# Cross-attention kernel: twelve value loads issued by GpSimd, and other slots for the loads of the first batch

## Chip, cores, metric

The kernel runs on one core of a Trainium2 chip. The metric is the device time of one execution in microseconds (us). Engines: TensorE (PE in the profile: matrix products), VectorE (DVE), ScalarE (ACT), GpSimd (POOL) and SyncE (SP), which only issues transfers. Each engine works through its own instructions in order; engines wait for each other by semaphores. Transfers (DMA) are issued by SyncE or by GpSimd, each into its own queue, and are carried by 16 DMA engines.

## What is computed

```python
# x: (8, 256, 1024), ctx: (8, 256, 1024), 32 heads of 32, all float32
h = (x - mean(x)) * rsqrt(var(x) + 1e-5) * gamma + beta
Q = split_heads(h @ Wq.T)              # K = V = split_heads(ctx)
scores = einsum('bhsd,bhtd->bhst', Q, K) * 32 ** -0.5
scores = where(mask, scores, -inf)
probs = softmax(scores)
attn = einsum('bhst,bhtd->bhsd', probs, V)
out = x + merge_heads(attn) @ Wout.T
```

## The kernel before

Work goes in **quads**: four heads of one batch, 8 quads a batch, 64 in all, numbered n = 0 to 63. The main loop has one iteration per quad; iteration n computes the scores of quad n+1 on TensorE, then its softmax, and the values product (probabilities times V, `values`, L823) of older quads. Between these stand the query products of the next batch, the output products of the last one, and the preparation of later batches: load of x, statistics (`ln_stats`), normalisation (`ln_norm`), block transposes (`blocks_x`), sixteen moves between partitions (`move_x`). The order on each engine is the order in which the Python program issues the instructions; it is written out by hand, and a table `PLAN` at the top of the file says in which iteration ("slot") each load, sum and move stands and which engine does it.

**Softmax of a quad** (`softmax_parts`, L663): for each of its four heads VectorE adds the mask and takes the row maximum (L687), ScalarE takes the exponential and its sum (L691), VectorE the reciprocal (L701), GpSimd the scaling (L707; fifty heads of the plan are scaled by ScalarE, L705), VectorE a transpose by blocks (L713). ScalarE copies one half aside (L719, `pc`), and four transfers swap quarters between partitions (L793): two `pT<-pT`, and, once these have landed, two `pT<-pc`. Only then is a quad's `pT` ready for the values product. Loads of the iteration come in two lists: `ahead`, issued right after the last normalisation of the softmax and ahead of the swaps, and `between`, issued between the two pairs of swaps. For quads 1 to 7, and again in the last batch, the last transpose, the swaps and `between` are held back into the next quad's softmax (`tails`).

**Values.** From quad 8 on, V of two quads (n, n+1; 512 KB) comes by one load (`load_v`, L286) into one buffer, `v_all`, which there is once (`vp`: 1). For quads 8 to 53 the plan's `pairs` lets odd iterations run the values products of two quads together (`values_pair(n - 3)`), and `vlate` puts the load of quads n, n+1 (n from 8 to 54) into `ahead` of iteration n+1, that is right behind the products that read the buffer before. It must have landed two iterations later; for quad 54, which is worked alone, one. Quads 0 to 7 have a load of 256 KB each, into one half of the buffer; quads 56 to 63 use another buffer.

**Who issues a load.** Every load, move and store has a key, and `issue` (L247) looks it up in the plan's `qp`: 0 (not listed) is SyncE (L252), 1 is GpSimd at that place of the program (L254), 2 is GpSimd at the end of the iteration (L1323). Loads of values of quads 24 to 55 share keys by their number modulo 8, since `per(n)` gives "%0" to "%7" there; `v%0` is listed with 1, so quads 24, 32, 40 and 48 are loaded by GpSimd.

**The first batch.** `woload` lists loads of output weights as [which, pair, slot]: `which` is 0 for the block B11, 1 for B21, 2 for B22, 3 for B12; a slot below 0 is before the loop, behind the loads of query weights. In slots 3 and 4 the two loads of B21 are added. Sums of these blocks run on GpSimd from slot 4 on. `b2` holds the slots of batch 2's preparation: loads, statistics, norms and transposes of the two halves of x, and the sixteen moves. `rs0` holds the slots of the four loads of residual rows of batch 0, counted from 8; the rows are used by VectorE and GpSimd in iterations 10 to 14. All these loads stand in `between`.

```python
ahead = [partial(load_v, n)] if ... and n not in V_EARLY and str(n) not in V_LATE else []
if V_LATE.get(str(n - 1)) == 'a':
    ahead.append(partial(load_v, n - 1))
...
for load in ahead:
    load()
```

Of the kernel before, what the change touches and what calls it, by code (L numbers as in the profile page):

```python
# [53 lines left out]
 'folds': 'PPPPPPPP',  # L54
 'b2': {'loads': [0, 1],
        'stats': [2, 4],
        'norms': [2, 4],
        'trans': [3, 5],
        'moves': [5, 5, 5, 5, 5, 5, 5, 6, 6, 6, 6, 6, 7, 7, 7, 7]},
 'b3': {'loads': [-14, -11],  # L60
        'stats': [-10, -9],
        'norms': [-9, -8],
# [11 lines left out]
         'norms': [-9, -8],  # L74
         'trans': [-8, -7],
         'moves': [-7, -6, -6, -6, -6, -6, -6, -5, -5, -5, -4, -4, -4, -4, -4, -4]},
 'woload': [[2, 1, 0], [3, 0, 3], [0, 1, 1], [0, 0, 3], [3, 1, 2], [2, 0, 2]],
 'n11': 'V',
 'p1late': [0],
 'qp': {'out00': 2,  # L80
# [39 lines left out]
        'x2_0None': 1,  # L120
        'ring3_B110': 2,
        'mv2_11': 1,
        'r1_11': 2},
 'vearly': {'62': 'b', '60': 'z'},
 'rs': [0, 1, 1, -3],
 'rs0': [-1, 1, 1, 1],
 'bufs': {'ptp': 4, 'vp': 1, 'asp': 2},
 'vsplit': 8,
 'pairs': [11, 13, 15, 17, 19, 21, 23, 25, 27, 29, 31, 33, 35, 37, 39, 41, 43, 45, 47, 49, 51, 53, 55],
# [1302 lines left out]
```

## Time and profile before

| | us |
|---|---|
| plain runs, median of 3 | 580.47 (579.62 to 581.26) |
| profiled execution, its time | 583.7 |
| profiled execution, span from first to last instruction | 581.9 |

Times in the profile count from the first instruction. A row of the timeline has the start, the length, the engine, the line, the operation, written and read tiles, shapes, the number of instructions merged, and in brackets how long the engine had stood idle and what ended that. `SPq` marks SyncE's issues: the length is the issue's own, not the transfer's. `pv` is the result of the values product, `wo` output weights, `ring` and `kept` parts of weights moved out and in, `sc` scores, `r` residual rows, `xnT<-xe` the moves of x.

### The profile page before, as it was taken

How to read it: one execution, taken by the hardware profiler on the slowest of the kernel's cores; microseconds unless marked ns; L12 is line 12 of the kernel's file. 1: busy time of each engine (PE TensorE's matmuls, PEld its weight loads, DVE VectorE, ACT ScalarE, POOL GpSimd, SP SyncE). 2: the span in 40 equal slices, each digit the busy share in tenths (PEclk: the TensorE clock that was granted, in tenths of full speed). 3: DMA queues.
4: the chain of work that ended last, by engine and by line, in shares of the span. 5: the costliest groups of instructions: out<-in, count | busy, mean ns of one | idle time of the engine just before them, and what ended most of it. 6: DMA issues, size and time to landing. Idle time of an engine off the chain costs nothing.

```text
span 581.9 us, 19975 instructions
## 1 busy us (share of the span) xinstructions
PE 566.3 (97%) x7162; PEld 397.5 (68%) x7162; DVE 463.4 (80%) x1700; ACT 450.5 (77%) x1524; POOL 397.2 (68%) x637
## 2 busy tenths in 40 slices
PE   8999899999999999999999999999899999999997
PEld 8787776766676777577666776677566776754543
DVE  5899888888888799898788888888856879679823
ACT  4699988887798977888678897789668788879920
POOL 1579987869867886967577673877916865257680
PEclk9999999999999999999999999999989999999999
DMA  8578967766876778777885788867785666645651
GB/s 315 215 203 231 264 181 212 203 179 168 239 220 200 200 204 261 213 202 201 226 245 162 205 240 235 241 171 192 174 239 154 206 179 200 160 113 164 188 159 74
DMA packets 45908, 116.94 MB, mean 201 GB/s; under 512 B 9136, under 2 KB 9904, under 8 KB 45808
## 3 DMA queue, kind: packets, MB, share of 16 engines
q1 hardware_dynamic: 39808, 96.50, 58.9%
q0 software_dynamic: 5712, 19.14, 11.0%
q8 instruction: 57, 0.93, 0.7%
q14 instruction: 43, 0.35, 0.2%
q10 hardware_dynamic: 288, 0.01, 0.0%
HBM read 64.23 MB, written 11.53 MB: 130 GB/s over the span
## 4 chain that ended last, share of the span: by engine, by line
PE 59%; DMA 12%; DVE 9%; ACT 7%; POOL 5%; issue 4%; SPq 3%; DVEq 0%; POOLq 0%
PE po_S L923 13%; PE pq_A L608 9%; PE po_A L923 8%; PE pv L833 8%; PE sc L647 7%; PE pq_S L608 6%; PE pq L506 6%; DMA pT<-pT 5%; DVE e L687 4%; DMA v_all<-in_kv_dram 4%; POOL e L707 4%; ACT e L691 4%; PE po_end L990 2%; DVE pT L713 2%; SPq L252 2%
## 5 line engine op out<-in xcount | busy, mean ns | idle before, releaser
L707 POOL TENSOR_SCALAR e<-e,rden 128x256 f32<-128x256 f32 x412 | 191.6, 480 | 135.3 <-DVE rden L701 129.5
L691 ACT ACTIVATE e<-e,mn 128x256 f32<-128x256 f32 x512 | 253.8, 503 | 29.9 <-DVE mn L687 29.2
L713 DVE STREAM_TRANSPOSE pT<-e 128x512 f32<-128x512 f32 x256 | 180.8, 708 | 52.9 <-POOL e L707 26.9
L687 DVE CUSTOM_DVE_ANT_0 e<-sc,mb 128x256 f32<-128x256 f32 x512 | 185.3, 415 | 13.2 <-PE sc L647 12.3
L719 ACT COPY pc<-pT 128x512 f32<-128x512 f32 x128 | 78.8, 617 | 47.2 <-DVE pT L713 32.1
L691 ACT ACTIVATION_READ_ACCUMULATOR e<-e,mn 128x1 f32 x512 | 99.4, 194 | 0.0
L506 PE MATMUL pq<-xnT,wq 128*128 128x256 f32 (+1 forms) x368 | 84.0, 382 | 0.0
L506 PEld LDWEIGHTS pq<-xnT,wq 128*128 128x128 f32 x368 | 68.8, 190 | 14.7 <-issue 4.4
L647 PE MATMUL sc<-k,qa 32*128 32x256 f32 x1024 | 73.8, 401 | 0.1
L923 PE MATMUL po_S<-wo,at 128*128 128x512 f32 x152 | 73.7, 606 | 0.2 <-ACT ends L941 0.2
L647 PEld LDWEIGHTS sc<-k,qa 32*128 32x128 f32 x1024 | 45.9, 184 | 39.4 <-issue 21.1
L833 PE MATMUL pv<-pT,v_all 64*32 64x128 f32 x3584 | 62.9, 278 | 7.6 <-DMA v_all<-in_kv_dram 4.9
L833 PEld LDWEIGHTS pv<-pT,v_all 64*32 64x32 f32 x3584 | 53.7, 107 | 19.7 <-issue 8.7
L923 PE MATMUL po_A<-wo,at 128*128 128x512 f32 x128 | 58.5, 602 | 0.1
L701 DVE RECIPROCAL rden<-den 128x2 f32<-128x2 f32 x256 | 38.0, 148 | 22.1 <-ACT e L691 21.8
L923 PE MATMUL po_S<-wo,s 128*128 128x512 f32 x104 | 49.3, 605 | 0.2 <-DVE r L965 0.2
L705 ACT ACTIVATE e<-e,rden 128x256 f32<-128x256 f32 x100 | 45.0, 501 | 1.6 <-DVE rden L701 1.6
L608 PEld LDWEIGHTS pq_A<-xnT,wq 128*128 128x128 f32 x352 | 41.0, 192 | 5.3 <-issue 4.5
L923 PEld LDWEIGHTS po_S<-wo,at 128*128 128x128 f32 x152 | 26.0, 190 | 24.2 <-issue 23.6
L687 DVE DVE_READ_ACCUMULATOR2_ANT mn<- 128x1 f32 x512 | 42.4, 83 | 0.0
L923 PEld LDWEIGHTS po_A<-wo,at 128*128 128x128 f32 x128 | 23.3, 190 | 26.9 <-issue 23.8
L608 PE MATMUL pq_A<-xnT,wq 128*128 128x128 f32 x352 | 41.1, 275 | 0.0
(116 smaller groups left out, 682.6 us busy)
## 6 DMA issues: line engine op xcount, KB each, us to landing
pT<-pT SPq DMA_DIRECT2D x128, 128.0 KB, 3.7
pT<-pc SPq DMA_DIRECT2D x128, 128.0 KB, 3.6
v_all<-in_kv_dram SPq DMA_DIRECT2D x19, 512.0 KB, 5.3
k<-in_kv_dram SPq DMA_DIRECT2D x31, 256.0 KB, 4.2
r<-in_x_dram SPq DMA_DIRECT2D x26, 256.0 KB, 4.4
ring<-kept_T SPq DMA_DIRECT2D x11, 512.0 KB, 5.3
xnT<-xe SPq DMA_DIRECT2D x76, 64.0 KB, 3.3
out_dram<-r POOLq DMA_DIRECT2D x18, 256.0 KB, 3.6
```

The lines of the kernel that those rows point to most:

```text
L506: nc.tensor.matmul(pqs[n], wq[:, o, c, :], xnTs[b](c), start=(c == 0), stop=(c == NC - 1),)
L608: nc.tensor.matmul(pqs[b][:, o, :], w[:, c], x_[:, c], start=begins and o + c == 0, stop=c == NK - 1, skip_group_check=True,)
L647: nc.tensor.matmul(scs[n][j][:, s, :], qa[r, n % NQ, ts(s, P)], ks[n - n % 2][r, n % 2, :], start=True, stop=True,)
L687: nc.vector.tensor_tensor_reduce(out=e[:, s, :], in0=pss[j][:, s, :], in1=mbs[n // NQ], scale=1.0, scalar=NO_SCORE, op0=ALU.add, op1=ALU.m ...
L691: nc.scalar.activation(e[:, s, :], e[:, s, :], AF.Exp, bias=mn[:, s : s + 1], scale=-1.0, accum_out=den[:, s : s + 1],)
L701: nc.vector.reciprocal(rden, dens[j])
L705: engine.activation(es[j][:, s, :], es[j][:, s, :], AF.Copy, scale=rden[:, s : s + 1])
L707: engine.tensor_scalar(es[j][:, s, :], es[j][:, s, :], rden[:, s : s + 1], 1.0, ALU.mult, ALU.mult,)
L713: nc.vector.transpose(pT[:, :, :, j, :, :].rearrange("p a i s k -> p (a i) s k"), es[j].rearrange("p s (b t) -> p b s t", t=K),)
L719: nc.scalar.copy(pc[:, :, ts(j, 2)], pT[:, 1, :, ts(j, 2)])
L833: nc.tensor.matmul(pvs[n][r][j * HD : (j + 1) * HD], vs[n - n % 2][ts(r, 2 * K), n % 2, i, ts(j, HD)], pT[ts(r, 2 * K), :, i, j, :, :], st ...
L923: nc.tensor.matmul(po, operand(b, name)[:, c], wo[:, which, c], start=begins and c == 0, stop=c == NK - 1, skip_group_check=not begins,)
```

## The change

Only the table `PLAN` changes; the program that reads it is the same. The values of quads 26, 28, 30, 34, 36, 38, 42, 44, 46, 50, 52 and 54 (with the quad after each) are issued by GpSimd. Of the output weights' loads, B12's first pair goes from slot 3 to before the loop, B12's second from slot 2 to 1, B22's second from slot 0 to 2. The second half of batch 2's x is loaded in slot 0 (was 1), its statistics and norm stand in slot 3 (was 4), the first half's transpose in slot 4 (was 3); of the moves, six, six and four stand in slots 5, 6 and 7 (were seven, five and four). The residual rows of batch 0 are loaded in slots 8, 8, 10 and 11 (were 7, 9, 9 and 9).

```diff
- 'b2': {'loads': [0, 1],
-        'stats': [2, 4],
-        'norms': [2, 4],
-        'trans': [3, 5],
-        'moves': [5, 5, 5, 5, 5, 5, 5, 6, 6, 6, 6, 6, 7, 7, 7, 7]},
+ 'b2': {'loads': [0, 0],
+        'stats': [2, 3],
+        'norms': [2, 3],
+        'trans': [4, 5],
+        'moves': [5, 5, 5, 5, 5, 5, 6, 6, 6, 6, 6, 6, 7, 7, 7, 7]},
...
- 'woload': [[2, 1, 0], [3, 0, 3], [0, 1, 1], [0, 0, 3], [3, 1, 2], [2, 0, 2]],
+ 'woload': [[0, 0, 3], [3, 1, 1], [3, 0, -1], [0, 1, 1], [2, 0, 2], [2, 1, 2]],
...
-        'r1_11': 2},
+        'r1_11': 2,
+        'v%2': 1,
+        'v%4': 1,
+        'v%6': 1},
...
- 'rs0': [-1, 1, 1, 1],
+ 'rs0': [0, 0, 2, 3],
```

## The prediction

> **What bounds the kernel now.** I read the page's engine sums first, then the groups of TensorE, then TensorE's timeline for every place where it stood still.
>
> ```profile
> span 581.9 us, 19975 instructions
> PE 566.3 (97%) x7162; PEld 397.5 (68%) x7162; DVE 463.4 (80%) x1700; ACT 450.5 (77%) x1524; POOL 397.2 (68%) x637
> L833 PE MATMUL pv<-pT,v_all 64*32 64x128 f32 x3584 | 62.9, 278 | 7.6 <-DMA v_all<-in_kv_dram 4.9 <-DMA pT<-pT 1.5 <-ACT e L705 1.0
> ```
>
> TensorE is busy for 566.3 of 581.9 us, so no edit of loads can win more than its idle 15.6 us (and what its clock loses). Half of that, 7.6 us, stands ahead of one group: the values products, mostly for the value load. One by one, with the stall in brackets:
>
> ```profile
> 59.65 1.25 PE L833 MATMUL pv<-pT,v_all 64*32 64x128 f32 x64 [0.48 <-DMA pT<-pT]
> 68.37 1.25 PE L833 MATMUL pv<-pT,v_all 64*32 64x128 f32 x64 [1.01 <-ACT e L705]
> 84.60 1.26 PE L833 MATMUL pv<-pT,v_all 64*32 64x128 f32 x64 [0.98 <-DMA v_all<-in_kv_dram]
> 282.16 2.31 PE L833 MATMUL pv<-pT,v_all 64*32 64x128 f32 x128 [0.98 <-DMA pT<-pT]
> 368.40 2.20 PE L833 MATMUL pv<-pT,v_all 64*32 64x128 f32 x128 [0.91 <-DMA v_all<-in_kv_dram]
> 402.19 2.13 PE L833 MATMUL pv<-pT,v_all 64*32 64x128 f32 x128
> 422.46 3.87 PE L833 MATMUL pv<-pT,v_all 64*32 64x128 f32 x128 [2.33 <-DMA v_all<-in_kv_dram]
> 501.79 1.36 PE L833 MATMUL pv<-pT,v_all 64*32 64x128 f32 x64 [0.66 <-DMA v_all<-in_kv_dram]
> 422.80:426.20 3.40, 3.40 (x127) 0.50 0.84 234
> ```
>
> The first three are quads 3, 4 and 6; then come the pairs that begin with quads 28, 38 and 44, and quad 54. The last row (a window of TensorE: length, busy, granted clock, DMA share, GB/s) shows that after the 2.33 us stop the clock stood at 0.50 for 3.40 us, which costs half of it, 1.70 us: that pair took 3.87 us where an undisturbed one takes 2.13.
>
> **Why these loads are late.** A value load waits only for the pair before it to be read. SyncE issued those loads here:
>
> ```profile
> 277.29 0.53 SPq L252 DMA_DIRECT2D v_all<-in_kv_dram  x1
> 362.96 0.40 SPq L252 DMA_DIRECT2D v_all<-in_kv_dram  x1
> 410.79 3.67 SPq L793 DMA_DIRECT2D pT<-pc  x2
> 414.50 2.46 SPq L252 DMA_DIRECT2D xnT<-xe  x3
> 417.00 0.58 SPq L252 DMA_DIRECT2D v_all<-in_kv_dram  x1
> 497.22 0.54 SPq L252 DMA_DIRECT2D v_all<-in_kv_dram  x1
> ```
>
> For quad 44 the buffer was free at 402.19 + 2.13 = 404.32, but the load stood behind the swaps of another quad (410.79) and three moves, and went out at 417.00, 12.7 us later. Nothing about its own data held it.
>
> **The change: values of quads 24 to 55.** Twelve loads (26, 28, 30, 34, 36, 38, 42, 44, 46, 50, 52, 54) leave SyncE; the four at multiples of 8 were GpSimd's already. In GpSimd's order each stands right behind the normalisation of the quad two ahead, as the trace shows for a load that it has now (219.25 + 1.85 = 221.10, load at 221.04):
>
> ```profile
> 219.25 1.85 POOL L707 TENSOR_SCALAR e<-e,rden 128x256 f32<-128x256 f32 x4 [0.53 <-DVE rden L701]
> 221.04 0.58 POOL L254 DMA_DIRECT2D v_all<-in_kv_dram  x1
> 268.29 2.88 POOL L707 TENSOR_SCALAR e<-e,rden 128x256 f32<-128x256 f32 x6 [0.55 <-DVE rden L701]
> 358.21 0.94 POOL L707 TENSOR_SCALAR e<-e,rden 128x256 f32<-128x256 f32 x2 [4.27 <-ACT e L705]
> 407.22 2.89 POOL L707 TENSOR_SCALAR e<-e,rden 128x256 f32<-128x256 f32 x6 [0.54 <-DVE rden L701]
> 495.79 0.94 POOL L707 TENSOR_SCALAR e<-e,rden 128x256 f32<-128x256 f32 x2 [0.83 <-DVE rden L701]
> ```
>
> So the new issue times are 271.2, 359.2, 410.1 and 496.7: earlier by 6.1, 3.8, 6.9 and 0.5 us. Time from issue to landing, loads of SyncE from 232 us on, then those of GpSimd from 205 us on (minimum, median, maximum):
>
> ```profile
> DMA to landing us min/median/max: 4.1/5.3/8.6
> DMA to landing us min/median/max: 3.8/4.7/5.9
> ```
>
> With 4.7 us they land at 275.9, 363.9, 414.8 and 501.4. TensorE was ready at 281.18, 367.49, 420.13 and 501.13 (start less stall), so the first three stalls go: 0.98 + 0.91 + 2.33 = **4.2 us**, and the half clock with them, **1.7 us**. Quad 54 keeps 0.3 of 0.66: **0.4 us**. What is late next there: for quad 45 the swap back, of which the second went out near 414 and landed after some 3.6 us, ahead of 420.13; so I let TensorE run on.
>
> ```profile
> pT<-pc SPq DMA_DIRECT2D x128, 128.0 KB, 3.6
> DVE pT L713 <- POOL e L707: 26.9, 94, 1.4
> ```
>
> Twelve issues like that at 221.04, 0.58 us each, add 7.0 us to GpSimd. Behind each wait the sums for the products and the next quad's normalisation, and for that VectorE's transposes, which wait for GpSimd 26.9 us in all now. I cost it at nothing: the cover is GpSimd's 32% idle and the lead of several us that transposed probabilities have on TensorE. Without it the price is up to 0.58 us a load, 7.0 in all. SyncE gains 12 x 0.53 = 6.4 us, which I also count as nothing. Where SyncE was prompt the new issue is later, and this bounds the edit from the other side:
>
> ```profile
> 318.29 2.11 PE L833 MATMUL pv<-pT,v_all 64*32 64x128 f32 x128
> 323.42 0.53 SPq L252 DMA_DIRECT2D v_all<-in_kv_dram  x1
> 324.50 0.94 POOL L707 TENSOR_SCALAR e<-e,rden 128x256 f32<-128x256 f32 x2 [1.01 <-DVE rden L701]
> 333.45 1.79 PE L833 MATMUL pv<-pT,v_all 64*32 64x128 f32 x106
> ```
>
> Quad 34 (and alike 26, 42, 50, once per batch): buffer free at 320.40, SyncE at 323.42, GpSimd at 325.4; needed at 333.45. There is room for 8.0 us of landing, against 4.7 at the median and 5.9 at most for GpSimd. I take no loss.
>
> **The change: the head.**
>
> ```profile
> 20.00:25.00 5.00, 5.00 (x35) 3.87 (x34) 4.15 (x13) 1.73 (x5) 3.19 (x7) 1.00 0.34 136
> 55.00:60.00 5.00, 4.52 (x50) 3.49 (x56) 4.88 (x19) 3.81 (x14) 4.37 (x10) 1.00 1.04 227
> 55.38 2.29 SPq L252 DMA_DIRECT2D wo<-in_woT_dram  x3
> 60.29 1.15 SPq L793 DMA_DIRECT2D pT<-pc  x2
> 70.97 5.19 SPq L252 DMA_DIRECT2D xnT<-xe  x7
> 76.26 1.16 SPq L793 DMA_DIRECT2D pT<-pT  x2
> 81.26 0.54 SPq L252 DMA_DIRECT2D v_all<-in_kv_dram  x1
> 60.15 1.24 ACT L413 ACTIVATE x<-x,shift,rstd 128x1024 f32<-128x1024 f32 x1 [1.04 <-POOL shift L410]
> ```
>
> One 512 KB load of output weights moves from the group of three at 55.38 to the end of the loads before the loop, where the DMA engines then work at 0.34 (20 to 25 us) and not at 1.04 (55 to 60). In between, x and weights only trade places: one such load per quad either way. At 227 GB/s the 0.52 MB less is 2.3 us less queue ahead of quad 4's swap back (60.29) and its value load, so its stall of 1.01 goes if that were all. But the second half of batch 2's x is now normalised a quad earlier, 1.24 us on ScalarE ahead of quad 5's exponentials and the swap of quad 4, which gives part back: I take 0.6. Moves in the first group fall from seven to six: at 5.19 / 7 = 0.74 us each that swap (76.26) and quad 6's value load (81.26) come earlier by at least that, and by the shorter queue before them: 0.9 of the 0.98. Quad 3's 0.48 stays. Head: **1.5 us**; bounds 2.0 (both stalls) and a loss of 1.2 (the ScalarE step on the path). The residual rows (before: one at quad 7's slot, three at quad 9's; after: two at 8, one each at 10 and 11) still have about two quads, some 15 us, against 8.6 us for the slowest of the larger loads above, and cost nothing; without that lead it would be one wait of that order.
>
> **Sum.** 4.2 + 1.7 + 0.4 + 1.5 = 7.8 us off the profiled execution's own 583.7 us: 575.9. That execution is 3.2 us over the median of the plain runs, 580.47. The item that is likeliest to be a matter of one execution is quad 44's stop with its half clock, 4.0 us; without it 3.8 us remain, 576.7 from the median; with it 572.7. I take **575.8**, nearer the former, since 583.7 - 4.0 = 579.7 is about what the plain runs show. Own range 572.5 to 578.5.
>
> **Rivals.**
> 1. Head worth nothing or a small loss, values as forecast. For it: ScalarE's added 1.24 us; against: the DMA share of 1.04. 580.47 - (0.98 + 0.91 + 0.4) = 578.2, or 574 with quad 44's; say 577.5.
> 2. The waits only change their name: the load is early and the swaps, or a normalisation delayed by 0.6 us, end at the same moment. For it: the stall at 282.16 is put down to a swap. Against: the swaps' lead worked out above. 580.
> 3. Slower: the loads of the four short intervals come late. Each has 8.0 us; past that TensorE waits once per batch. SyncE's loads took up to 8.6, GpSimd's up to 5.9, so the row is against it. At 9.8 us it would be 4 x 1.8 = 7.2 us, less 2.1 for the small stalls cured: 585.5; with nothing else gained it turns to a loss from 8.5 us on.
> 4. Slower: the head's ScalarE step and a shifted queue cost 2 us or more, and the plain runs never had quad 44's stop: 582.5.
>
> The Trainium skill speaks for the third (SBUF — State Buffer, "SBUF: two separate sides"): descriptors of a load issued from GpSimd are written by GpSimd, which certain VectorE operations lock out; its example grows from 620 to 3100 ns. By that, an estimate, a load would land 2.5 us later, at about 7.2 us, still short of 8.0. The trace does not agree so far: the loads from GpSimd landed no later than SyncE's.
>
> **How the numbers follow.** Forecast 0.52, rivals 0.16, 0.12, 0.12, 0.08. From no change one can tell 0.3%, 1.7 us: faster is below 578.7, slower above 582.2. The forecast and most of the first rival are faster: 0.64; the second and their edges the same: 0.16; the third and fourth slower: 0.20. The range 572.5 to 583.0 leaves out the third rival and a gain beyond all stalls, under 2 in 10.
>
> **What would show it.** Right: no stall at the pairs of quads 28, 38 and 44, value loads issued within 7 us of the pair's end, no window at half clock, seven 512 KB value loads left on SyncE, the stalls of quads 4 and 6 under 0.5 us. Wrong: stalls at the pairs of 26, 34, 42 or 50, GpSimd's loads landing after more than 8 us, or VectorE's wait for GpSimd growing by more than 7 us with TensorE idle for scores.

## The result, and the profile after

| | before | after |
|---|---|---|
| plain runs on one chip, median of 22 each (us) | 579.9 (577.25 to 588.23) | 577.35 (575.28 to 580.62) |
| ratio of the runs, 95% interval | | 0.9951 [0.9932, 0.9970] |
| profiled execution: time, span (us) | 583.7, 581.9 | 577.82, 576.0 |

The change makes the kernel faster by 0.5%, 2.8 us in plain runs (the forecast was 4.7). The ratio goes by the means of the runs without the few executions in a slower state, so it differs a little from that of the medians, which lie 2.55 us apart. In the code after the change, lines stand three lower than before: the values products of L833 are L836, SyncE's issue of L252 is L255. Some of the kernels below shift by none or by up to six lines; the texts of the rows say which step is meant.

From the page of the kernel after: the span, the engine sums, the group of the values products and the issues of value loads by GpSimd.

```profile
span 576.0 us, 19987 instructions
PE 566.6 (98%) x7162; PEld 397.0 (69%) x7162; DVE 463.1 (80%) x1700; ACT 449.3 (78%) x1524; POOL 402.9 (70%) x649
...
L836 PE MATMUL pv<-pT,v_all 64*32 64x128 f32 x3584 | 60.9, 273 | 0.8 <-ACT e L708 0.8
...
v_all<-in_kv_dram POOLq DMA_DIRECT2D x17, 512.0 KB, 5.1
```

TensorE's work is the same (566.6 against 566.3 us busy), so the span fell by idle time. Ahead of the values products 0.8 us of it is left, of 7.6. The timeline, load and product in turn, for the pairs that begin with quads 28, 38 and 44, and for quad 54:

```profile
271.31 0.58 POOL L257 DMA_DIRECT2D v_all<-in_kv_dram  x1
280.36 2.11 PE L836 MATMUL pv<-pT,v_all 64*32 64x128 f32 x128
...
356.55 0.59 POOL L257 DMA_DIRECT2D v_all<-in_kv_dram  x1
365.91 2.11 PE L836 MATMUL pv<-pT,v_all 64*32 64x128 f32 x128
...
407.44 0.61 POOL L257 DMA_DIRECT2D v_all<-in_kv_dram  x1
416.49 2.12 PE L836 MATMUL pv<-pT,v_all 64*32 64x128 f32 x128
...
489.34 0.60 POOL L257 DMA_DIRECT2D v_all<-in_kv_dram  x1
493.82 1.39 PE L836 MATMUL pv<-pT,v_all 64*32 64x128 f32 x64
```

None of these products has a bracket any more: each load now goes out some 9 us ahead of its use (4.5 for quad 54), and the pair of quad 44 takes 2.12 us where it took 3.87, with no stop and no half clock before it.

One stop is new in this execution, at quad 61 near the end. The timeline, and TensorE's window behind it (length, busy and counts of PE, PEld, DVE, ACT, POOL, then granted clock, DMA share, GB/s):

```profile
534.50 1.11 SPq L807 DMA_DIRECT2D x_again<-in_x_dram  x2
...
538.41 1.15 SPq L796 DMA_DIRECT2D pT<-pc  x2
...
545.66 2.06 PE L836 MATMUL pv<-pT,wq 64*32 64x128 f32 x64 [1.88 <-DMA wq<-in_kv_dram]
```

```profile
546.30:549.70 3.40, 3.40 (x64) 1.98 (x42) 0.00 (x0) 2.21 (x6) 3.37 (x5) 0.51 0.65 149
```

The bracket names a load of values that had gone out at 532.64, but the product begins 0.14 us behind the landing of the first swap back. The swaps back issued from 538.41 on landed at 545.5 and 545.9: after 7 us, behind the 1 MB of `x_again` that SyncE had issued 4 us ahead of it. The stop of 1.88 us was again followed by 3.40 us at half clock.

Twelve more issues on GpSimd were to cost nothing. Of the waits in the kernel after, VectorE's transposes for GpSimd (sum, count, longest):

```profile
DVE pT L716 <- POOL e L710: 29.2, 75, 4.4
```

It was 26.9 before and is 26.6 in the kernel that has only the values edit, so the 2.3 us more do not come from these issues. The experiments say where they come from.

### The profile page after: what moved, and what is told of

Read it like the earlier page. It is cut to its first block, busy times and chain, and to the rows that moved or that the text cites. A ratio compares the mean times of both kernels' runs of the same rounds, so it can differ in the third digit from the quotient of the medians.

```text
span 576.0 us, 19987 instructions
## 1 busy us (share of the span) xinstructions
PE 566.6 (98%) x7162; PEld 397.0 (69%) x7162; DVE 463.1 (80%) x1700; ACT 449.3 (78%) x1524; POOL 402.9 (70%) x649
## 4 chain that ended last, share of the span: by engine, by line
PE 66%; DVE 9%; POOL 8%; ACT 5%; issue 5%; DMA 5%; SPq 2%; DVEq 0%; POOLq 0%; ACTq 0%
PE po_S L926 15%; PE pq_A L611 13%; PE pv L836 8%; PE sc L650 8%; PE po_A L926 7%; PE pq L509 6%; POOL e L710 5%; PE pq_S L611 5%; DVE e L690 4%; PE po_end L993 3%; ACT e L694 3%; DVE pT L716 2%; DMA pT<-pT 2%; DMA xnT<-xe 1%; SPq L255 1%
## 5 line engine op out<-in xcount | busy, mean ns | idle before, releaser
L710 POOL TENSOR_SCALAR e<-e,rden 128x256 f32<-128x256 f32 x412 | 190.4, 476 | 118.8 <-DVE rden L704 112.8
L716 DVE STREAM_TRANSPOSE pT<-e 128x512 f32<-128x512 f32 x256 | 180.7, 708 | 58.0 <-POOL e L710 29.2
L836 PE MATMUL pv<-pT,v_all 64*32 64x128 f32 x3584 | 60.9, 273 | 0.8 <-ACT e L708 0.8
L836 PEld LDWEIGHTS pv<-pT,v_all 64*32 64x32 f32 x3584 | 51.7, 105 | 12.7 <-issue 8.2
L926 PEld LDWEIGHTS po_A<-wo,at 128*128 128x128 f32 x128 | 23.3, 190 | 26.9 <-issue 25.0
```

The lines of the kernel that those rows point to most:

```text
L710: engine.tensor_scalar(es[j][:, s, :], es[j][:, s, :], rden[:, s : s + 1], 1.0, ALU.mult, ALU.mult,)
L716: nc.vector.transpose(pT[:, :, :, j, :, :].rearrange("p a i s k -> p (a i) s k"), es[j].rearrange("p s (b t) -> p b s t", t=K),)
L836: nc.tensor.matmul(pvs[n][r][j * HD : (j + 1) * HD], vs[n - n % 2][ts(r, 2 * K), n % 2, i, ts(j, HD)], pT[ts(r, 2 * K), :, i, j, :, :], st ...
L926: nc.tensor.matmul(po, operand(b, name)[:, c], wo[:, which, c], start=begins and c == 0, stop=c == NK - 1, skip_group_check=not begins,)
```

## Experiments

Each ratio is against the kernel before, run on the same chip among the runs of its group; the medians of before were 580.45, 581.02 and 581.62 us for the first four kernels, the next four and the last four.

### The two halves of the change alone

`values_only`: the kernel before with the three keys `v%2`, `v%4`, `v%6`. `head_only`: the rest of the change without them.

```diff
-        'r1_11': 2},
+        'r1_11': 2, 'v%2': 1, 'v%4': 1, 'v%6': 1},
```

> The kernel before with only the twelve value loads issued by GpSimd; the head as before. Theory (each part brings its own): the stalls of the pairs of quads 28, 38 and 44 and the half clock go, those of quads 3, 4 and 6 (0.48, 1.01, 0.98 us) stay; ratio to the kernel before 0.996 to 0.998 in plain runs. Rival (the gain came from the head, the loads only changed the name of the wait): the pairs' stalls go but swaps or scores stop TensorE by as much; ratio 0.999 to 1.001. Rival (loads from GpSimd late in the short intervals): stalls at the pairs of quads 26, 34, 42 or 50, ratio over 1.

> The kernel before with only the head's slots changed (weights, rows, batch 2's x); values of quads 24 to 55 as before. Theory: stalls of quads 3, 4 and 6 fall from 2.5 us in all to about 0.8, the pairs of quads 28, 38 and 44 still stop TensorE by 1 to 4 us in all; ratio 0.997 to 0.999. Rival (the head brings nothing): ratio 1.000 and the same three stalls.

Measured: values_only 575.66 us, ratio **0.9911 [0.9882, 0.9941]**, which is 5.2 us less; head_only 582.81 us, ratio **1.0044 [1.0021, 1.0067]**, 2.6 us more. Neither expectation was met (0.996 to 0.998 and 0.997 to 0.999). The two add up to the change (0.9951). So the values edit alone is better than the whole, and the head, which was to gain 1.5 us, costs 2.6.

Where does the head lose? Not at its own place. In all four kernels run so far that have the head's new slots (after, head_only and the two of the next parts) TensorE stops at 170 to 175 us, ahead of the first query product of batch 3 (`pq_S`). The timeline of values_only, then of head_only: SyncE's swaps of quad 15, GpSimd's load of the second half of batch 4's x, GpSimd's first sum of batch 3's moved x, VectorE's and ScalarE's steps behind it, and the product.

```profile
142.83 1.14 SPq L796 DMA_DIRECT2D pT<-pT  x2
143.60 0.60 POOL L1326 DMA_DIRECT2D x<-in_x_dram  x1
145.07 1.28 SPq L796 DMA_DIRECT2D pT<-pc  x2
...
161.39 1.29 POOL L599 TENSOR_TENSOR sx<-xnT 128x512 f32<-128x512 f32 x1 [3.31 <-DMA pT<-pc]
...
164.98 0.71 DVE L716 STREAM_TRANSPOSE pT<-e 128x512 f32<-128x512 f32 x1 [1.39 <-POOL e L710]
...
168.25 0.48 ACT L522 ACTIVATE qa<-pq,qa 128x256 f32<-128x256 f32 x1
...
170.93 3.73 PE L611 MATMUL pq_S<-sx,ring 128*128 128x128 f32 x32
```

```profile
143.06 0.60 POOL L1323 DMA_DIRECT2D x<-in_x_dram  x1
143.79 1.15 SPq L793 DMA_DIRECT2D pT<-pT  x2
149.08 1.25 SPq L793 DMA_DIRECT2D pT<-pc  x2
...
161.99 1.52 SPq L252 DMA_DIRECT2D xnT<-xe  x1
...
165.37 1.26 POOL L596 TENSOR_TENSOR sx<-xnT 128x512 f32<-128x512 f32 x1 [7.84 <-DMA pT<-pc]
...
168.92 0.71 DVE L713 STREAM_TRANSPOSE pT<-e 128x512 f32<-128x512 f32 x1 [5.88 <-POOL e L707]
...
169.71 0.91 ACT L705 ACTIVATE e<-e,rden 128x256 f32<-128x256 f32 x2 [4.03 <-DVE rden L701]
...
171.91 0.46 ACT L519 ACTIVATE qa<-pq,qa 128x256 f32<-128x256 f32 x1
...
172.51 3.81 PE L608 MATMUL pq_S<-sx,ring 128*128 128x128 f32 x32 [1.43 <-POOL shift L410]
```

The swaps back (`pT<-pc`) go out only when the first swaps have landed. In values_only that is 2.2 us behind them, in head_only 5.3, and there the 512 KB load of x stands in front of the swaps. Behind the swaps back in SyncE's order stand the last moves of batch 3's x; the last goes out at 161.99 (158.56 in values_only). GpSimd waits for it, 7.84 us instead of 3.31. The bracket of the sum names a swap back; but the sum reads what the moves write, and in the eleven traces that have the landing of that last move it begins 0.38 to 0.39 us behind it.

How the late sum stops TensorE takes a closer look, since the sums themselves end at 167.97, 4.5 us before the product begins. Behind its sums GpSimd does its scalings of the softmax. VectorE's transposes wait for those (5.88 us instead of 1.39), so its reciprocals `rden` come late, and ScalarE waits for them 4.03 us. Behind that stands ScalarE's copy `qa<-pq,qa`. It reads out the query product before this one, and the program has one buffer for these results (`ps_q`), so the new product must wait for it. The copy ends at 172.37 (at 168.73 in values_only, well ahead of the product), and in all six traces with the stop TensorE's wait for ScalarE ends 0.03 to 0.04 us behind this copy. The bracket at the product names GpSimd's `shift` instead, which ends 0.07 to 0.08 us behind the copy in the same six traces; the product reads nothing of `shift`. VectorE's longer waits for GpSimd in the kernel after, 29.2 us, come from here too: the longest of them, 4.4 us, ends at 167.30.

### The same value loads, later on GpSimd

`values_end` is the kernel after with the twelve loads at the end of GpSimd's iteration.

```diff
-        'v%2': 1, 'v%4': 1, 'v%6': 1},
+        'v%2': 2, 'v%4': 2, 'v%6': 2},
```

> The changed kernel with the twelve loads issued by GpSimd at the end of the iteration, behind its sums, and not right behind the normalisation. Theory (what counts is when the load goes out): issue 8 to 9 us after the buffer is free and not 5, so in the short intervals (quads 26, 34, 42, 50) landing at 13 to 14.5 us against 13.1 needed: stalls of 0 to 1.5 us there, ratio 0.996 to 1.000. Rival (what counts is that SyncE is rid of the loads): no new stalls, ratio as for the changed kernel, 0.994 to 0.996.

Measured: 582.36 us, ratio 1.0031 [1.0000, 1.0061]. The timeline of values_end, and TensorE's window behind the product:

```profile
365.24 0.55 POOL L1326 DMA_DIRECT2D v_all<-in_kv_dram  x1
...
372.69 3.53 PE L836 MATMUL pv<-pT,v_all 64*32 64x128 f32 x128 [2.51 <-issue]
```

```profile
373.20:376.60 3.40, 3.40 (x118) 3.02 (x98) 0.81 (x7) 0.36 (x3) 2.50 (x4) 0.50 0.74 194
```

The load of quad 38 went out at 365.24 (356.55 in the kernel after), and the stop with its half clock is back. Same engine, same twelve loads, another place: what the values edit gains is the earlier time of issue, not that GpSimd does it. The stops did not come where they were expected: the pairs of 26, 34, 42 and 50 have none, those of 30, 38 and quad 54 have 1.44, 2.51 and 1.32 us. And the loads are not the whole of the difference, since this profile also stops 1.67 us ahead of `pq_S` (0.47 after).

### The stop at quad 61

`again_early` is the kernel after with `x_again` loaded four iterations earlier.

```diff
-        if n == N - 4:
+        if n == N - 8:
```

> The changed kernel with the second load of the last batch's x (x_again, two of 512 KB) in iteration 56 and not 60. Theory (the changed kernel gives part of its gain back in the tail, where these loads stand between the two pairs of swaps of quad 61): the swaps back of quad 61 land some 3 us earlier, the stop of 1.88 us at quad 61 and the half clock behind it (1.7 us) go; span about 573, ratio 0.990 to 0.993. Rival (that stop was one execution's): the profile has no such stop but the plain runs stay at 0.994 to 0.996.

Measured: 581.16 us, ratio 0.9995 [0.9965, 1.0026]. The stop at quad 61 was gone, as expected, but the time did not fall (0.990 to 0.993 was expected): TensorE now waited 1.23 us for a load of K at 523.78. The larger lesson is in the kernels that leave the end as it was: none of the other twelve profiles shows a stop over 0.52 us at quad 61. The stop belonged to one execution, and there was next to nothing to win. The profile of again_early shows the stop at batch 3's product larger than after, though both have the same instructions up to there:

```profile
143.84 0.60 POOL L1326 DMA_DIRECT2D x<-in_x_dram  x1
144.27 1.15 SPq L796 DMA_DIRECT2D pT<-pT  x2
...
174.70 3.48 PE L611 MATMUL pq_S<-sx,ring 128*128 128x128 f32 x29 [1.86 <-POOL shift L413]
```

### Which of the head's edits

Four kernels: the change with the residual rows in their old slots (`rows_back`), and the values edit with one of the head's three edits each.

```diff
rows_back   (after)         - 'rs0': [0, 0, 2, 3],     + 'rs0': [-1, 1, 1, 1],
values_rows (values_only)   - 'rs0': [-1, 1, 1, 1],    + 'rs0': [0, 0, 2, 3],
values_wo   (values_only)   woload as after
values_b2   (values_only)   b2 as after
```

The theory here was that the rows, loaded two and three slots later, push SyncE back.

> The kernel after with the four residual rows of batch 0 back in slots 7, 9, 9, 9. Theory (rows): the rows at slots 10 and 11 delay SyncE, batch 3's last move goes out some 3 us later, GpSimd waits for it (6.37 us idle at 163.74 in the kernel after, 3.31 with the values edit alone), and TensorE stops before the first query product of batch 3. With the rows back that stop near 170 us is gone, GpSimd's wait is 3 to 4 us, and the ratio to the kernel before is 0.988 to 0.991: the gains of the weights' and x slots at quads 4 and 6 come on top of the values edit's 0.991. Rival (x and moves of batch 2, or the weights' loads): the stop stays, ratio 0.993 to 0.997.

> The values edit and the residual rows' new slots, the rest of the head as before. Theory (rows): the stop at the first query product of batch 3 is there, 0.4 to 1.8 us, GpSimd's wait before it is over 5 us, ratio 0.994 to 0.999. Rival: no such stop, ratio 0.989 to 0.993 as with the values edit alone.

> The values edit and the output weights' new slots, the rest of the head as before. Theory (rows): no stop at 170 us; the stops of quads 4 (0.48 with the values edit alone) and 6 (0.54) fall or stay, ratio 0.988 to 0.992. Rival (the weights' loads did the harm): the stop at 170 us is there, ratio 0.994 to 0.999.

> The values edit and batch 2's new slots for x, statistics, transpose and moves, the rest of the head as before. Theory (rows): no stop at 170 us, ratio 0.988 to 0.993. Rival (ScalarE's step a quad earlier and the moves shifted did the harm): the stop at 170 us is there or new ones before 80 us, ratio 0.994 to 0.999.

| | us | ratio | GpSimd's wait ahead of its sum | stop ahead of `pq_S` |
|---|---|---|---|---|
| rows_back | 576.72 | 0.9914 [0.9879, 0.9948] | 8.11 | 0.99 |
| values_rows | 578.06 | 0.9938 [0.9909, 0.9967] | 5.91 | 0 |
| values_wo | 574.95 | 0.9889 [0.9846, 0.9931] | 3.58 | 0 |
| values_b2 | 577.18 | 0.9934 [0.9903, 0.9966] | 5.91 | 0 |

The theory fell: with the rows back the stop was still there, and rows alone and batch 2's slots alone each lengthened GpSimd's wait, although neither has a load or a move near 145 us. In both, the scores of quad 20 start some 0.6 us later against those of quad 19 than in values_only, though the timeline names no stop. Only the weights' slots did no harm. What the two have in common is SyncE's lag against GpSimd by a few tenths of a us when both come to 143 us. In plain runs rows_back is faster than the kernel after (0.9914 against 0.9951, the intervals overlap), although its profile stops longer: one profile does not say how often a kernel meets the stop.

### The collision itself

The new theory: what decides is which goes out first, SyncE's swaps of quad 15 or GpSimd's load of batch 4's x. Two kernels have the load moved back by two normalisations (`x_later` from after, `head_x_later` from head_only), one has it moved ahead by one sum in the kernel with the values edit alone (`x_early`), and `wo_x_later` is values_wo with the load moved back.

```diff
+        'x4_1None': 5,
...
+        elif mode == 5:
+            nexts.append((2, partial(nc.gpsimd.dma_start, to, of)))
...
-        issue(f'x{pb(b)}{s}{h}', xs[b][:, s, cols], x[b, ts(s, P), cols])
+        issue(f'x{pb(b, 5)}{s}{h}', xs[b][:, s, cols], x[b, ts(s, P), cols])
```

```diff
-        for one in sums[n]:
+        for k, one in enumerate(sums[n]):
+            if n == 14 and k == len(sums[n]) - 1:
+                at_end.pop(0)()
             one()
```

> The kernel after, and GpSimd issues the load of the second half of batch 4's x two normalisations later (some 2.3 us). Theory (race): in all traces with the stop before batch 3's first query product this 512 KB load goes out ahead of a half swap of quad 15, or at most 0.1 us behind it, and that swap then lands 4.5 to 7 us after its issue instead of 2.2; SyncE's queue stands behind it. With the load 2 us behind both half swaps they land after 2.2 to 2.5 us, GpSimd's wait ahead of its sum falls from 6.4 to 3 to 4 us, the stop of 0.43 at 170 us goes, ratio 0.990 to 0.994 (0.9951 before). Rival (SyncE is late because of what the head's rows and moves did to its own order): the wait stays over 5.5 us, ratio as before, 0.994 to 0.997.

> The head's new slots alone, and the same later load of batch 4's x. Theory (race): the stop of 1.39 at 171 us is gone and most of the head's loss with it, ratio 0.999 to 1.002 (1.0044 with the head alone). Rival: stop and ratio stay, 1.003 to 1.006.

> The values edit alone, and GpSimd issues the load of batch 4's x one sum earlier, 1.3 us, so that it is ahead of both half swaps of quad 15. Theory (race): both swaps land 5 us or more after their issue, GpSimd's wait ahead of its sum is 7 to 8.5 us (3.31 in the values edit alone), a stop of 1 to 2 us at 170 us comes up without any edit of the head, ratio 0.994 to 0.998 (0.9911 in the values edit alone). Rival: no stop, ratio 0.989 to 0.993.

> The values edit, the output weights' new slots and the later load of batch 4's x: the candidate for the best version. Theory (race): in the values edit with the new weights' slots the swaps had a lead of only 0.5 us over the load, so that some executions may lose it; with the later load none does: ratio 0.985 to 0.989, GpSimd's wait at most 3.6 us. Rival: no change against 0.9889.

| | us | ratio | without the load's edit |
|---|---|---|---|
| x_later | 574.38 | 0.9895 [0.9857, 0.9934] | after: 0.9951 [0.9932, 0.9970] |
| head_x_later | 579.53 | 0.9972 [0.9945, 1.0000] | head_only: 1.0044 [1.0021, 1.0067] |
| x_early | 577.09 | 0.9934 [0.9905, 0.9962] | values_only: 0.9911 [0.9882, 0.9941] |
| wo_x_later | 575.35 | 0.9904 [0.9871, 0.9938] | values_wo: 0.9889 [0.9846, 0.9931] |

The timeline of x_early, in which no edit of the head is left, and then of x_later, which has all of them:

```profile
142.21 0.60 POOL L1325 DMA_DIRECT2D x<-in_x_dram  x1
142.46 1.14 SPq L796 DMA_DIRECT2D pT<-pT  x2
148.38 1.30 SPq L796 DMA_DIRECT2D pT<-pc  x2
...
164.87 1.27 POOL L599 TENSOR_TENSOR sx<-xnT 128x512 f32<-128x512 f32 x1 [6.91 <-DMA pT<-pc]
...
172.03 3.81 PE L611 MATMUL pq_S<-sx,ring 128*128 128x128 f32 x32 [1.04 <-POOL shift L413]
```

```profile
143.25 1.14 SPq L799 DMA_DIRECT2D pT<-pT  x2
146.34 1.14 SPq L799 DMA_DIRECT2D pT<-pc  x2
146.57 0.60 POOL L704 DMA_DIRECT2D x<-in_x_dram  x1
...
163.24 1.27 POOL L602 TENSOR_TENSOR sx<-xnT 128x512 f32<-128x512 f32 x1 [5.65 <-DMA pT<-pc]
...
170.65 3.73 PE L614 MATMUL pq_S<-sx,ring 128*128 128x128 f32 x32
```

Moving one load by 1.3 us makes the stop without the head, and moving it back takes the stop away with the head in place. All profiles side by side (in the first column, how much later than the second first-swap the load was issued; a minus means that the load was ahead; in the second, from that swap's issue to the issue of the swap back that waits for it; in the last, from TensorE's first scores product of quad 16 to its first of quad 24):

| | load behind swap, us | until the swap back, us | GpSimd's wait, us | stop, us | quad 16 to 24, us |
|---|---|---|---|---|---|
| wo_x_later | 3.98 | 2.49 | 3.65 | 0 | 73.5 |
| x_later | 2.76 | 3.13 | 5.65 | 0 | 74.6 |
| head_x_later | 2.57 | 2.83 | 5.22 | 0 | 74.2 |
| before | 0.49 | 2.37 | 3.29 | 0 | 73.4 |
| values_wo | 0.48 | 2.35 | 3.58 | 0 | 73.4 |
| values_only | 0.22 | 2.47 | 3.31 | 0 | 73.4 |
| values_b2 | 0.05 | 4.54 | 5.91 | 0 | 74.8 |
| after | -0.07 | 5.16 | 6.37 | 0.47 | 75.2 |
| values_rows | -0.17 | 4.66 | 5.91 | 0 | 74.8 |
| values_end | -0.37 | 6.19 | 8.05 | 1.67 | 77.0 |
| x_early | -0.80 | 6.16 | 6.91 | 1.04 | 75.8 |
| again_early | -0.98 | 6.91 | 9.22 | 1.86 | 78.2 |
| rows_back | -1.21 | 5.86 | 8.11 | 0.99 | 77.0 |
| head_only | -1.28 | 5.48 | 7.84 | 1.43 | 76.8 |

With the load 0.2 us or more behind, the swap back follows within 2.35 to 3.13 us; with the load at most 0.05 us behind, or ahead, within 4.54 to 6.91. The three kernels after, values_end and again_early have the same instructions up to here and still differ by 0.9 us in the first column, so the order is settled anew in each execution.

The last column has the whole price, of which the stop is only a part. In the four profiles in which the swap back follows within 2.5 us, TensorE takes 73.4 to 73.5 us for the eight quads. In the eight with the collision it takes 74.8 to 78.2, which is 1.4 to 4.8 us more, also in the two whose timeline names no stop. In head_only it is 3.4 us more than before; plain runs of that kernel lose 2.6.

Not all expectations were met. GpSimd's wait stayed at 5.65 us in x_later (3 to 4 were expected) and at 5.22 in head_x_later, and the eight quads take 1.2 and 0.8 us more than in values_only. In x_later a part of it is the load again, at its new place: of the swaps back (146.34, two) the first went out ahead of the load (146.57) and landed after 2.3 us, the second went out 0.37 us behind it and landed only at 153.44, after 6.5 us. SyncE's next load of values, which waited for that landing, went out at 153.52. What the rest comes from was not traced. The lag is not enough for the stop. But GpSimd's sums of query weights are still late behind it, and the product that uses them takes 4.3 us in x_later (1.95 and 2.38) where it takes 3.73 in values_only. In the timeline of x_later:

```profile
198.07 1.95 PE L614 MATMUL pq_A<-sx,wq 128*128 128x128 f32 x16
200.17 2.38 PE L614 MATMUL pq_A<-sx,wq 128*128 128x128 f32 x16 [0.15 <-POOL wq L563]
```

In x_early the ratio alone does not prove the loss, since its interval holds that of values_only in part (0.9905 to 0.9941); its trace does. And wo_x_later gained nothing over values_wo, against the expectation: where the swaps already led, a later load of x was worth nothing. That makes the two gains above those of the collision, not of the load's new place as such. (The intervals of head_only and head_x_later lie apart; those of after and x_later just touch.)

Of the versions, values_wo (0.9889), x_later (0.9895), wo_x_later (0.9904) and values_only (0.9911) are all faster than both kernels by their medians; their intervals overlap, so the runs do not rank them.

## Why the prediction came out right

The time is inside the forecast's own range, 1.5 us above the forecast. In part that is luck. The forecast for plain runs is 4.7 us below the kernel before, of which the head is 1.5 and so the values are 3.2. Measured alone, the values gain 5.2, which is 2.0 more than that, and the head loses 2.6, which is 4.1 worse than forecast and of the other sign. The first error makes up for half of the second. The mechanism of the values was understood, that of the head was not.

The first rival, "head worth nothing or a small loss, values as forecast", names what the halves show, and its 577.5 us is nearer to the measured 577.35 than the forecast. It had a chance of 0.16, and its reason for the loss, ScalarE's added 1.24 us at the start, is not the one that the runs show.

**Values, forecast 6.3 us in the profiled execution, 2.3 to 6.3 in plain runs: measured 5.2 in plain runs.** Mechanism and size hold. The stops at the pairs of 28, 38 and 44 are gone, and the load of quad 44 went out 5.7 us behind the pair before it (401.7 to 407.44) instead of 12.7. The choice on plain runs, that quad 44's stop with its half clock may be a matter of one execution and weighs little, was too careful: 5.2 us are more than the small stops' 2.3 alone.

**GpSimd's twelve issues, costed at nothing.** Right: in values_only VectorE's wait for GpSimd is 26.6 us against 26.9.

**The short intervals (third rival).** No stop at the pairs of 26, 34, 42 or 50. The load of quad 34 was issued at 322.90, landed at 328.85 and was used at 330.98. GpSimd's loads of values from 250 us on landed after 4.0, 5.1 and 7.8 us (least, median, most): the most (quad 36's, which has more time) is close to the 8.0 us of room that the short intervals have, so the rival was nearer than the 5.9 before let it seem. The Trainium skill (SBUF — State Buffer, "SBUF: two separate sides") says that a load issued from GpSimd waits for its descriptors while certain operations of VectorE run; by the prediction's estimate from the example there the median would have been 7.2. The trace does not agree: it has 5.1.

**The head, forecast 1.5 us gained: measured 2.6 us lost (head_only). This is the step that failed**, with its sentence that the residual rows "cost nothing" and with the cover of the shifted queue, which was followed to quad 6's load and no further. What the runs show in its place has two parts.

First, the gain itself may be about as forecast once the collision is out of the way: head_x_later is at 0.9972 [0.9945, 1.0000], 1.6 us less, with 0 to 3.2 in the interval, and a part of the collision is left in it. But the stops from which it was worked out are not fixed numbers. Up to the first of the rows' slots (slot 7) values_rows has the same instructions as before, and values_only up to quad 24. Their timelines at quads 4 and 6, where before showed 1.01 and 0.98, values_only first:

```profile
67.80 1.25 PE L836 MATMUL pv<-pT,v_all 64*32 64x128 f32 x64 [0.51 <-ACT qa L518]
...
83.61 1.35 PE L836 MATMUL pv<-pT,v_all 64*32 64x128 f32 x64 [0.57 <-ACT pc L722]
```

```profile
66.55 1.25 PE L836 MATMUL pv<-pT,v_all 64*32 64x128 f32 x64
...
81.78 1.16 PE L836 MATMUL pv<-pT,v_all 64*32 64x128 f32 x64
```

With all of the head in place, the kernel after still shows 0.81 at quad 4 (67.83) and none at quad 6. A term made of sub-microsecond stops in one execution is known no better than this spread. Larger ones come and go too: near 355 us the query product `pq_A` stands still for 2.45 us in again_early, 1.51 in values_only and not at all in rows_back, each time waiting for nothing that the profile shows.

Second, the loss came far behind the head: the stop stands at 171 us, the last of the head's loads (residual rows) went out at 118.8. The prediction's rule was to follow each queue that a step is moved past, and it was not followed far enough: SyncE came to quad 15's swaps a few tenths of a us later against GpSimd, and a load that goes out just behind them in the profiles of before and values_only went out just ahead. The collision is shown by the three kernels that move only that load. That the lag comes from the rows and from batch 2's slots rests on one profile for each alone. It is borne out by the others: with the load in its old place, the three profiles with neither edit have it 0.22 us or more behind the swap, the seven with one or both at most 0.05. The path by which slots 0 to 8 reach 143 us was not traced step by step and stays open.

**Other rivals.** That the waits only change their name does not hold: of 7.6 us ahead of the values products 0.8 are left. The fourth, a shifted queue in the head that costs 2 us or more, was right about the head's sign and its size (2.6) and wrong about its cause (not ScalarE's step) and about the rest: it assumed that the plain runs never had quad 44's stop. Of what would show it wrong, "VectorE's wait for GpSimd growing" was the right place to look: it grew by 2.3 us, a third of the threshold, and by 6.6 in head_only (33.5).

## What to carry to other kernels

In a kernel at 98% of its bound, a moved load can be paid for wherever its queue next meets another engine's queue within a few tenths of a us. Look in the trace of before for small transfers that lead a large one by less than half a us, and name them as risks even when the edit is far away; then take the knife-edge out by moving the large one, and far enough: in x_later it met the next swap. A stop under 1 us read from one execution is a draw, not a price: compare two profiles of the same instructions before building a term on it. And split a change in two on the chip even when the sum is as forecast: here the better half was worth nearly twice the whole.

## What the hardware did that was not expected

A 512 KB load issued 0.07 us ahead of a swap of 128 KB more than doubled the time until the swap back that waits for it went out (5.16 us against 2.47 with the load 0.22 us behind), although two different engines issued the load and the swap. The stops of 1.88 us (after), 2.51 (values_end) and 2.33 (before) were each followed by 3.40 us at half clock. The stop of 1.86 us in again_early ahead of the query product was not: its next 3.40 us ran at the full clock.

```profile
174.70:178.10 3.40, 3.40 (x30) 3.40 (x31) 3.33 (x14) 2.96 (x7) 2.66 (x3) 1.00 1.00 336
```

That is the same window of TensorE (granted clock 1.00, ahead of the DMA share and GB/s). Nor was the stop of 2.45 us in the same execution, at 359.19 (1.00 from 356 to 362 us). So the length of a stop alone did not decide.
